# Tokens in two layouts: first blocks scaled by rows in place of transposed, another order of down products, keys in another bank

## The chip, the cores and the metric

The kernel runs on one core of one Trainium2 chip. The metric is the device time of one execution in microseconds (us). Three runs of the kernel before gave 3192.99, 3193.81 and 3198.65 us; their median, 3193.81 us, is the time before.

## The reference

Eight sequences of 512 tokens with 512 features pass through a macaron block: a gated feed-forward part, attention, and the same feed-forward part again, all in float32, with a layernorm ahead of each.

```python
def _layernorm(x, axis=-1, eps=1e-05):
    m = jnp.mean(x, axis=axis, keepdims=True)
    v = jnp.var(x, axis=axis, keepdims=True)
    return (x - m) / jnp.sqrt(v + eps)
...
    h = jax.nn.silu(jnp.einsum('bsh,hi->bsi', x, w_gate)) * jnp.einsum('bsh,hi->bsi', x, w_up)
    h_sparse = _sparsify_2to4(h)
    return jnp.einsum('bsi,ih->bsh', h_sparse, w_down)
...
    x = x + 0.5 * _L0_ffn_ref(_layernorm(x, axis=-1), L0_ffn_w_gate, L0_ffn_w_up, L0_ffn_w_down)
    x = x + _L0_attn_ref(_layernorm(x, axis=-1), L0_attn_W_q, L0_attn_W_k, L0_attn_W_v, L0_attn_W_o)
    x = x + 0.5 * _L0_ffn_ref(_layernorm(x, axis=-1), L0_ffn_w_gate, L0_ffn_w_up, L0_ffn_w_down)
```

The feed-forward part has 2048 hidden features; of each four neighbours the two of largest magnitude are kept. Attention has 16 query heads and 4 key/value heads of 32 features, with rotary positions.

## The kernel before

**Blocks and chunks.** There are 16 feed-forward blocks: for each sequence b a first one (before attention, `i = 0`) and a second one (`i = 1`). `blocks` (L95) gives their order. Places 0 to 3, 5, 8, 9 and 11 are first blocks, whose input is the kernel's own input x. Between the groups of matmuls of a block, "sides" are interleaved: the attention of an earlier sequence and the layernorm of the next block.

A block works through four chunks of 512 hidden features. Per chunk, gate and up are made in two stretches (`woven`, L633) of seven products each instead of eight, in the manner of Strassen and Winograd: the tokens' half blocks `b11`, `b21`, `b22` and four differences of them (`ts`, made by `sums`, L331) are multiplied by quarters of the weights and by sums of quarters. The results are put together in the tiles `row` and `corner`. VectorE then prunes (`keep_two_of_four`, L407; its last step is L454), one half of the tokens after the other. When the second half is done, GpSimd makes three sums `e` and one in place in h (L460 to L463).

Two chunks at a time go through the down projection, again as seven products (`products`, L544, in the order of `PRODUCTS`, L488). Each line of that table names the side taken from h (two digits: token half, feature half) or from e (0, 1, 2), the weights, the accumulating bank (x, v or z), and the quarter of the output that the bank is added to afterwards. A bank goes on accumulating over several products, so a product waits until the add (`add`, L581, operation on L583) that read the bank before it is done. The seven products of a pair of chunks are `owed`, and are worked off at the end of the chunk after it (L777), of the last pair in the first chunk of the next block. `load_x` brings the residual into the only buffer of its pool at the end of a block's first chunk (L778). Three weight tiles are in flight; each product issues the load of the third one after it.

**Layernorm.** `layernorm_t` (L280) is a generator with one step a `yield`. For a first block (tag "xf") it loads four tiles of 128 tokens, takes the moments on VectorE (L297), makes scale and bias in a chain of 12 small operations on GpSimd twice (`scales`, L300), normalises on ScalarE (`normalise`, L314), transposes with 16 TensorE operations in four groups (`turn`, L318; the transposes are on L264), copies the groups from PSUM on ScalarE (L328) and makes the four differences on VectorE (`sums`, on L167). The result `xT` holds features on the partitions and tokens along the row. Only the first block of all has another path (`xb` given).

**What sets the order.** The order of instructions is written out by the program itself under a manual schedule. It keeps a plan of the time at which each engine would be free (`at`), and lets operations of VectorE join a queue: `soon` (urgent), `later` (put off) and the steps of the pruning. `fill` (L388) issues what fits before the planned time of TensorE. A side's next step is taken when its due place has come (`place`, `pace`, L1147 to L1176) and when its condition, the time it yielded, has passed in the plan. `WIDTH`, 42, is the length of a block in those units; a layernorm has 13 steps from 15 to 2 units ahead of its block. Engines execute their queues in order. All transfers are issued by SyncE (SP), also in order; 16 quarters of gate/up weights (`load_quarters`) are in flight.

**PSUM.** Three banks (`Bank`, L227) are shared by all short-lived results: gate/up and down products, transposes (`tr`), key projection (`proj`, L906), values (`vps`, L916) and the softmax denominators. One more bank (`acc_slots`) holds the attention's weighted sums (`ops`, L1071), four a sequence, and another four hold the scores.

Of the kernel before, what the change touches and what calls it, by code (L numbers as in the profile page):

```python
# [18 lines left out]
P = 128  # L19
# [7 lines left out]
def macaron_block(  # L27
    ctx: ExitStack,
    tc: tile.TileContext,
    x: bass.AP,  # L30
    w_gu: bass.AP,
    w_down: bass.AP,
    w_q: bass.AP,
# [74 lines left out]
    def load_quarters(*used):  # L108
# [3 lines left out]
        while coming and len(quarters) < QUARTERS:  # L112
# [4 lines left out]
            elif block != blocks[0]:  # L117
                nc.sync.dma_start(out=w, in_=gu_sums[i][:, q - S1])

    xs = {(0, 0): load_x(0, 0)}  # L120
    load_quarters()
    ident = const.tile([P, P], FP, name="ident")
# [56 lines left out]
    def waits(end):  # L179

        takes("pe", 0.0, end + TOLD)
# [95 lines left out]

    in_xT = []

    def layernorm_t(got, tag, src=None, xb=None):  # L280

# [49 lines left out]
        def sums():  # L331

            xT = got["xT"]
            (b11, b12), (b21, b22) = ([xT[:, 2 * i : 2 * i + 2, j * HALF : (j + 1) * HALF] for j in range(2)] for i in range(2))
            if tag == "xf":
                got["sums"] = ts = tp.tile([P, 4, 2, HALF], FP, tag="ts", name="ts")
            else:
                got["sums"] = ts = p_slots.tile([P, 4, 2, HALF], FP, "ts")
            got["made"] = [
                (later if tag == "xf" else soon)(  # L340
                    0.62, partial(nc.vector.tensor_tensor, ts[:, i], a, b, ALU.subtract), at["act"]
                )
                for i, a, b in ((0, b12, b11), (1, b22, ts[:, 0]), (2, b22, b12), (3, b21, ts[:, 1]))
            ]

        if xb is None:
            there = at["pe"] + 10.0
            yield lambda: there
            found = [soon(0.9, partial(moments, t)) for t in (0, 1)]
            yield now  # L350
            found += [soon(0.9, partial(moments, t)) for t in (2, 3)]
            yield partial(when, found[:2])
            ensure(found[:2])
            scales((0, 1))
            yield partial(when, found)
            ensure(found)
            scales((2, 3))
            yield by_scalar
            for t in range(NT):
                normalise(t)  # L360
                end = at["act"]
                yield by_scalar if t < NT - 1 else (
                    lambda: max(end, by_scalar()) if tag == "xa" or len(in_xT) < 2 else None
                )
            for t in range(NT):
                turn(t)
                yield by_scalar if t < NT - 1 else now
            sums()
        else:

            function(AF.Sqrt)
            for t in range(NT + 1):
                if t < NT:
                    moments(t)
                    va = rs[:, 0, t : t + 1]
                    nc.vector.tensor_scalar(va, mv[:, t, 1:2], EPS, None, ALU.add)
                    nc.scalar.activation(va, va, AF.Sqrt)
                if t:
                    i = t - 1
                    nc.vector.reciprocal(rs[:, 1, i : i + 1], rs[:, 0, i : i + 1])  # L380
                    nc.vector.tensor_scalar(
                        xn[i], xb[:, i, :], mv[:, i, 0:1], rs[:, 1, i : i + 1], ALU.subtract, ALU.mult
                    )
                    turn(i)
            function(AF.Silu)
            sums()
# [88 lines left out]
    def begin(steps):  # L475
# [58 lines left out]
    def ffn(b, final, last):  # L534
# [5 lines left out]
        def store(xb, ts):  # L540
            for t in ts:
                nc.sync.dma_start(out=done[t * P : (t + 1) * P, :], in_=xb[:, t, :])

        def products(hs, g):  # L544
# [8 lines left out]
            def product(i):  # L553
# [37 lines left out]
                written[b, final] = taken[name]  # L591

            for _ in range(3):
                load()
# [38 lines left out]
        def woven(h, i, r, last_one):  # L633
# [95 lines left out]
        for c in range(NCH):  # L729
# [19 lines left out]
            if last and c == NCH - 1:  # L749

                for half in range(2):
                    for r in range(4):
                        yield from hidden(h, 2 * c + r // 2, r, slice(half * HALF, (half + 1) * HALF))
                        if half == 1 and r >= 2:
                            yield from some(2)
                    begin(keep_two_of_four(h, [], e, range(half, half + 1)))
            else:
                for pair in range(2):
# [6 lines left out]
                        groups = woven(h, i, 2 * pair, last_one)  # L765
                    for k, g in enumerate(groups):
                        yield g
                        if k == 2 and opens and i + 1 < 2 * NCH:
                            combine_gu(i + 1)
                    if opens:  # L770
# [64 lines left out]
        return w  # L835

    def attention(b):
        ensure(written[b, 0])
        wkv = wap.tile([P, ND, 2 * KV], FP, tag="wa", name="wkv")
        coming_qo = deque([("q", q) for q in SEVEN_Q] + [("o", q) for q in SEVEN_O])  # L840
        weights = deque()
# [61 lines left out]
                yield partial(when, taken[order[i + 1]] if i < 6 else [])  # L903


        ps = Bank([P, S], "proj")  # L906
        for k in range(ND):
            nc.tensor.matmul(
                out=ps.tile, lhsT=wkv[:, k, :KV], rhs=xT[:, k, :], start=(k == 0), stop=(k == ND - 1)
            )  # L910
        multiplied(3.43)
        fill()
        read, of_k = rotated(kT, ps.tile, cs[:, 0, :], cs[:, 1, :], 1.0)
        ps.free(read)
        yield now
        vps = Bank([P, NT, KV], "vps")  # L916
        for t in range(NT):
# [229 lines left out]
    def place(b, i):  # L1147
        return WIDTH * blocks.index((b, i))
# [116 lines left out]
```

## Time and profile before

| what | value |
|---|---|
| median of three runs | 3193.81 us |
| the profiled execution, its own time | 3194.41 us |
| its span | 3192.6 us |
| granted TensorE clock (mean) | 0.999 |
| TensorE busy, weight loads busy | 3152.0 us, 2391.1 us |
| VectorE, ScalarE, GpSimd busy | 2256.3, 1176.2, 525.6 us |
| DMA: data moved, mean rate | 475.30 MB, 149 GB/s |
| token transposes (L264, float32) | 384 |

The profile describes one execution. Busy time is the time in which an engine had at least one instruction in flight. A matmul's records overlap, so the time that one occupies TensorE is the distance from its start to the start of the next. In a list of waits the columns are: who waited, for whom, the sum, the number of waits and the longest one, in us. In a timeline they are: start, length, engine, line, operation, what it writes and reads, the number of instructions merged, and in brackets the idle time before it with what ended it.

### The profile page before, as it was taken

What the parts mean: (1) busy time and instruction counts of PE and PEld (TensorE: products, weight loads), DVE (VectorE), ACT (ScalarE), POOL (GpSimd) and SP (SyncE); (2) the same over time, 40 slices, a digit from 0 to 9 for tenths busy, and PEclk for the clock granted to TensorE, in tenths of its full rate; (3) what the DMA queues carried; (4) which work ended last, traced back from release to release, by engine and by line L of the source; (5) the groups of instructions that cost most, each with busy time, mean ns of one, the idle gap of its engine ahead of it and who ended that gap; (6) DMA issues with size and microseconds to landing.
All of it is one profiled execution on the core that took longest, in us unless ns stands there. A gap on an engine that the chain in (4) does not pass through costs nothing.

```text
span 3192.6 us, 43897 instructions
## 1 busy us (share of the span) xinstructions
PE 3152.0 (99%) x16264; PEld 2391.1 (75%) x16264; DVE 2256.3 (71%) x4458; ACT 1176.2 (37%) x1663; POOL 525.6 (16%) x822
## 2 busy tenths in 40 slices
PE   8999999999999999999999999999999999999999
PEld 6888667866787668766786678766876678667886
DVE  7767777588658776777658865877577766877554
ACT  2222443235422463244423542255324432454220
POOL 2322011211021102201121112111120112111110
PEclk9999999999999999999999999999999999999999
DMA  7773344534444436334453345443633445334541
GB/s 238 241 262 117 115 152 143 173 123 123 159 156 146 134 107 219 114 116 153 142 175 122 118 161 158 146 135 110 219 114 113 159 139 171 122 123 159 162 165 53
DMA packets 270069, 475.30 MB, mean 149 GB/s; under 512 B 26656, under 2 KB 82464, under 8 KB 269344
## 3 DMA queue, kind: packets, MB, share of 16 engines
q1 hardware_dynamic: 269856, 472.49, 46.4%
q8 instruction: 130, 2.13, 0.3%
q14 instruction: 83, 0.68, 0.1%
HBM read 432.54 MB, written 39.85 MB: 148 GB/s over the span
## 4 chain that ended last, share of the span: by engine, by line
PE 92%; DVE 4%; DMA 2%; POOL 1%; ACT 1%; issue 0%; SPq 0%; DVEq 0%; POOLq 0%; ACTq 0%
PE x L644 25%; PE v L644 13%; PE x L569 13%; PE v L569 7%; PE z L644 6%; PE seven L889 6%; PE st L1002 4%; PE sc L969 4%; PE ops L1018 4%; PE z L569 3%; PE tr L264 1%; PE gu L619 1%; PE vps L919 1%; PE den L1034 1%; PE st L1007 1%; PE y L602 1%
## 5 line engine op out<-in xcount | busy, mean ns | idle before, releaser
L644 PE MATMUL x<-ts,w 128*128 128x256 f32 x3000 | 717.1, 382 | 1.4 <-DVE corner L658 1.3
L644 PEld LDWEIGHTS x<-ts,w 128*128 128x128 f32 x3000 | 560.4, 190 | 130.5 <-issue 41.7
L460 POOL TENSOR_TENSOR e<-h 128x512 f32<-128x512 f32 x62 | 80.3, 1295 | 2154.4 <-DVE h L454 1982.8
L167 DVE TENSOR_REDUCE nm<-sc 128x1 f32<-128x512 f32 x512 | 321.6, 683 | 72.4 <-PE sc L969 70.8
L569 PE MATMUL x<-wd,h 128*128 128x256 f32 x1488 | 340.1, 382 | 0.8 <-DVE x L583 0.8
L569 PEld LDWEIGHTS x<-wd,h 128*128 128x128 f32 x1488 | 279.4, 190 | 61.6 <-issue 14.2
L167 DVE TENSOR_TENSOR total<-total,p 128x512 f32<-128x512 f32 x384 | 271.6, 743 | 73.0 <-ACT p L1010 73.0
L1010 ACT ACTIVATE p<-st 128x2048 f32<-128x2048 f32 x96 | 179.8, 1872 | 330.4 <-PE st L1007 289.5
L244 ACT COPY row<-x 128x512 f32<-128x512 f32 x203 | 118.8, 585 | 405.0 <-PE x L644 404.6
L256 ACT ACT_TABLE_LOAD x195 | 250.2, 1283 | 4.2 <-PEq L1254 0.7
L569 PE MATMUL v<-wd,e 128*128 128x256 f32 x992 | 230.3, 384 | 14.8 <-POOL e L460 11.5
L644 PE MATMUL v<-xT,w 128*128 128x256 f32 x1000 | 239.5, 382 | 2.9 <-ACT corner L244 1.5
L644 PE MATMUL x<-xT,w 128*128 128x256 f32 x1000 | 239.5, 382 | 1.8 <-ACT xT L328 1.8
L644 PE MATMUL z<-xT,w 128*128 128x256 f32 x1000 | 238.6, 381 | 0.0
L644 PE MATMUL v<-ts,w 128*128 128x256 f32 x1000 | 238.2, 381 | 0.0
L693 ACT ACTIVATE h<-x 128x256 f32<-128x256 f32 x125 | 47.6, 381 | 498.9 <-PE x L644 467.9
L569 PEld LDWEIGHTS v<-wd,e 128*128 128x128 f32 x992 | 187.2, 191 | 57.5 <-POOL e L460 14.7
L644 PEld LDWEIGHTS v<-xT,w 128*128 128x128 f32 x1000 | 186.7, 190 | 49.4 <-ACT row L244 8.0
L644 PEld LDWEIGHTS x<-xT,w 128*128 128x128 f32 x1000 | 186.2, 190 | 46.9 <-issue 20.6
L644 PEld LDWEIGHTS z<-xT,w 128*128 128x128 f32 x1000 | 187.1, 190 | 39.0 <-issue 15.0
L644 PEld LDWEIGHTS v<-ts,w 128*128 128x128 f32 x1000 | 187.6, 190 | 38.0 <-issue 8.9
L415 ACT ACTIVATE a<-h 128x1024 f32<-128x1024 f32 x128 | 134.9, 1054 | 159.5 <-DVE m L434 89.9
(129 smaller groups left out, 4564.6 us busy)
## 6 DMA issues: line engine op xcount, KB each, us to landing
w<-gu SPq DMA_DIRECT2D x472, 256.0 KB, 3.5
w<-in_w_gu SPq DMA_DIRECT2D x394, 256.0 KB, 3.4
wd<-wd SPq DMA_DIRECT2D x124, 512.0 KB, 5.4
wd<-in_w_down SPq DMA_DIRECT2D x186, 256.0 KB, 3.7
x<-x SPq DMA_DIRECT2D x64, 256.0 KB, 2.7
xn<-x SPq DMA_DIRECT2D x64, 256.0 KB, 4.5
x<-in_x SPq DMA_DIRECT2D x32, 256.0 KB, 3.6
gu<-w SPq DMA_DIRECT2D x32, 256.0 KB, 2.8
```

The lines of the kernel that those rows point to most:

```text
L167: self.does()
L244: nc.scalar.copy(dst, src)
L256: nc.scalar.activation(dummy[:, 1:2], dummy[:, 0:1], f)
L415: nc.scalar.activation(a, h[:, :, half * HALF : (half + 1) * HALF], AF.Abs)
L460: nc.gpsimd.tensor_tensor(sums[:, 0], h21, h22, ALU.add)
L569: nc.tensor.matmul(out=y.tile[:, t, :], lhsT=part[:, t * P : (t + 1) * P], rhs=operands[i][:, n, :], start=(first and t == 0 and n == 0), ...
L644: nc.tensor.matmul(out=bank.tile[:, m, :], lhsT=lhs[:, m, k, :], rhs=rhs[:, k, :], start=(first and m == 0 and k == 0), stop=(k == 1), ski ...
L889: nc.tensor.matmul(out=sc[:, bank, m, :], lhsT=lhs(w, i, m, k), rhs=rhs(w, i, k), start=(i in (0, 1, 5) and m == 0 and k == 0), stop=(k == 1),
L969: nc.tensor.matmul(out=sc[:, kv, :], lhsT=qT[rows, c, t * P : (t + 1) * P], rhs=kT[rows, :], start=True, stop=True)
L1002: nc.tensor.matmul(out=st[:, kv, :], lhsT=kT[rows, t * P : (t + 1) * P], rhs=qT[rows, c, :], start=True, stop=False)
L1010: nc.scalar.activation(p, st, AF.Exp)
L1018: nc.tensor.matmul(out=ops[rows, :], lhsT=v[:, t, rows], rhs=p[:, kv, :], start=(t == 0), stop=(t == NT - 1))
```

## The change

1. The host gives the input a second time, transposed (`x_t`: features on partitions, tokens along the row). The layernorm of the seven first blocks behind the very first one loads its token tiles for the moments as before, but no longer normalises and transposes them. It stores scale and bias per token in DRAM (`scales_of`, single elements of 4 bytes), loads `xT` from `x_t`, loads the 512 scales and the 512 biases back as rows copied to all 128 partitions, and lets VectorE multiply and add in place, eight operations of 128x512. These layernorms run four units earlier (`AHEAD`).
2. In `PRODUCTS` the product "12" x "21" moves from the sixth place to the second. The stores of a finished output half follow the fifth and the seventh product.
3. Six of the seven owed products are worked off at the end of a chunk; the seventh comes after the first gate/up product of the next stretch. The residual is loaded a chunk later.
4. The key projection goes to the accumulation bank in place of one of the three shared banks.

```diff
+    scales_of = {b: dram.tile([2, S], FP, name=f"scales_{b}") for b in range(B)}
...
+        def given_transposed():
+
+
+            yield lambda: at["pe"] if len(in_xT) < 2 else None
+            for i in range(2):
+                nc.sync.dma_start(out=scales_of[b][i].rearrange("(t p) -> p t", p=P), in_=rs[:, 1 + 2 * i, :])
+            in_xT.append(got)
+            got["xT"] = xT = xtp.tile([P, ND, S], FP, tag="xT", name="xT")
+            for c in range(ND):
+                nc.sync.dma_start(out=xT[:, c, :], in_=x_t[b][:, c, :])
+            there = at["pe"] + 5.0
+            yield lambda: there
+            rows = [xnp.tile([P, S], FP, tag=tag, name="rows") for _ in range(2)]
+            for i in range(2):
+                nc.sync.dma_start(out=rows[i], in_=scales_of[b][i].partition_broadcast(P))
+            there = at["pe"] + 5.0
+            yield lambda: there
+            got["normed"] = []
+            for c in range(ND):
+                got["normed"] += [
+                    later(0.62, partial(nc.vector.tensor_tensor, xT[:, c, :], xT[:, c, :], rows[i], op))
+                    for i, op in enumerate((ALU.mult, ALU.add))
+                ]
+                yield partial(when, got["normed"][-2:])
+            sums()
+            yield partial(when, got["made"])
+            yield now
...
             scales((2, 3))
+            if b is not None:
+                yield from given_transposed()
+                return
             yield by_scalar
...
         ("11", "11", "x", (0, 0)),
+        ("12", "21", "z", (0, 0)),
         (0, "12-11", "v", (1, 1)),
...
         ("21", "22-12", "x", (1, 1)),
-        ("12", "21", "z", (0, 0)),
         ("22", "21-T2", "x", (1, 0)),
...
-                    if g == NCH // 2 - 1 and i in (5, 6):
-                        store(xb, (0, 1) if i == 5 else (2, 3))
+                    if g == NCH // 2 - 1 and i in (4, 6):
+                        store(xb, (0, 1) if i == 4 else (2, 3))
...
+            waits(ensure(normed[b, final].pop("normed", ())))
             x = Bank([P, 2, HALF], "x")
...
                     for k, g in enumerate(groups):
                         yield g
+                        if k == 0 and len(owed) == 1:
+
+                            yield from some(1, False)
...
-                        yield from some(7, False)
-            if c == 0 and (b, final) not in xs:
+                        yield from some(6, False)
+            if c == 1 and (b, final) not in xs:
...
-        ps = Bank([P, S], "proj")
+        ps = acc_slots.tile([P, S], FP, "proj")
+        waits(acc_slots.ready)
...
-        ps.free(read)
+        acc_slots.used(read[0])
...
+    AHEAD = 4
...
-        stage = partial(layernorm_t, normed[b, i], "xf", tokens[b][2 * i])
-        sides.append((place(b, i) - 15, place(b, i) - 2, NORM, stage, ("attention", b) if i else None, None))
+        stage = partial(layernorm_t, normed[b, i], "xf", tokens[b][2 * i], b=None if i else b)
+        ahead = 0 if i else AHEAD
+        sides.append((place(b, i) - 15 - ahead, place(b, i) - 2 - ahead, NORM, stage, ("attention", b) if i else None, None))
...
+        "x_t": x.reshape(B, S, D // P, P).transpose(0, 3, 2, 1),
```

More of the change, by code (lines that the diff above doesn't have):

```diff
@@ L30, in macaron_block @@
     x: bass.AP,
+    x_t: bass.AP,
     w_gu: bass.AP,
@@ L278, in macaron_block, with layernorm_t @@
     in_xT = []
-    def layernorm_t(got, tag, src=None, xb=None):
+    def layernorm_t(got, tag, src=None, xb=None, b=None):
         if tag == "xf":
@@ L340, in sums @@
                 (later if tag == "xf" else soon)(
-                    0.62, partial(nc.vector.tensor_tensor, ts[:, i], a, b, ALU.subtract), at["act"]
+                    0.62, partial(nc.vector.tensor_tensor, ts[:, i], a, a2, ALU.subtract), at["act"]
                 )
-                for i, a, b in ((0, b12, b11), (1, b22, ts[:, 0]), (2, b22, b12), (3, b21, ts[:, 1]))
+                for i, a, a2 in ((0, b12, b11), (1, b22, ts[:, 0]), (2, b22, b12), (3, b21, ts[:, 1]))
             ]
+        def given_transposed():
[23 more added lines that the diff above has]
+            yield now
         if xb is None:
@@ L590, in product @@
                     y.free(taken[name])
-                written[b, final] = taken[name]
+                if i == len(PRODUCTS) - 1:
+                    written[b, final] = taken[name]
             for _ in range(3):
@@ L753, in ffn @@
                         yield from hidden(h, 2 * c + r // 2, r, slice(half * HALF, (half + 1) * HALF))
+                        if half == r == 0:
+                            yield from some(1, False)
                         if half == 1 and r >= 2:
@@ L767, in ffn @@
                         yield g
+                        if k == 0 and len(owed) == 1:
+                            yield from some(1, False)
                         if k == 2 and opens and i + 1 < 2 * NCH:
@@ L775, in ffn @@
                         begin(keep_two_of_four(h, list(last_one), e))
-                        yield from some(7, False)
-            if c == 0 and (b, final) not in xs:
+                        yield from some(6, False)
+            if c == 1 and (b, final) not in xs:
+                assert not owed
                 for entries in written.values():
@@ L837, in attention @@
     def attention(b):
-        ensure(written[b, 0])
+        ensure(written.pop((b, 0)))
         wkv = wap.tile([P, ND, 2 * KV], FP, tag="wa", name="wkv")
@@ L903, in seven @@
                 yield partial(when, taken[order[i + 1]] if i < 6 else [])
-        ps = Bank([P, S], "proj")
+        ps = acc_slots.tile([P, S], FP, "proj")
+        waits(acc_slots.ready)
         for k in range(ND):
             nc.tensor.matmul(
-                out=ps.tile, lhsT=wkv[:, k, :KV], rhs=xT[:, k, :], start=(k == 0), stop=(k == ND - 1)
+                out=ps, lhsT=wkv[:, k, :KV], rhs=xT[:, k, :], start=(k == 0), stop=(k == ND - 1)
             )
@@ L912, in attention @@
         fill()
-        read, of_k = rotated(kT, ps.tile, cs[:, 0, :], cs[:, 1, :], 1.0)
-        ps.free(read)
+        read, of_k = rotated(kT, ps, cs[:, 0, :], cs[:, 1, :], 1.0)
+        acc_slots.used(read[0])
         yield now
```

## The prediction

> **What bounds the kernel now.** I read the page's busy times and its chain first. They say whether a change must take work from TensorE or may only shift it.
>
> ```profile
> span 3192.6 us, 43897 instructions
> ...
> PE 3152.0 (99%) x16264; PEld 2391.1 (75%) x16264; DVE 2256.3 (71%) x4458; ACT 1176.2 (37%) x1663; POOL 525.6 (16%) x822
> ...
> PE 92%; DVE 4%; DMA 2%; POOL 1%; ACT 1%; issue 0%; SPq 0%; DVEq 0%; POOLq 0%; ACTq 0%
> ```
>
> TensorE is busy 99% of the span and is 92% of the chain, at a granted clock of 0.999. A microsecond of matmul time removed is a microsecond of span, unless a new wait takes its place. VectorE (71%) and ScalarE (37%) lie beside it. Second, the waits of TensorE, longest sums first:
>
> ```profile
> PE v L569 <- POOL e L460: 11.5, 8, 2.0
> PE tr L264 <- DVE xn L381: 7.6, 3, 6.5
> PE v L569 <- DMA wd<-in_w_down: 3.2, 1, 3.2
> PE st L1002 <- DVE nm L167: 3.1, 4, 1.8
> PE vps L919 <- DVE kT L167: 2.4, 3, 0.8
> PE x L644 <- ACT xT L328: 1.8, 2, 0.9
> ```
>
> All listed waits add up to 36 us. The largest is the second down product, which needs e, GpSimd's sum, made by L460. The 7.6 us are the program's start, which the change leaves alone. Third, the timeline shows the price of what is removed, and then one of the eight waits for e:
>
> ```profile
> 132.10 0.60 PE L264 MATMUL tr<-ident,xn 128*128 128x128 f32 x4
> 132.54 1.89 PE L644 MATMUL z<-xT,w 128*128 128x256 f32 x8
> 134.27 0.60 PE L264 MATMUL tr<-ident,xn 128*128 128x128 f32 x4
> 134.70 1.89 PE L644 MATMUL x<-ts,w 128*128 128x256 f32 x8
> ```
>
> Matmuls are pipelined, so I go by start to start, not by the 0.60 shown: four transposes hold TensorE for 0.44 us (132.10 to 132.54) and 0.43 us (134.27 to 134.70). A gate/up product takes 1.73 us in the same way (132.54 to 134.27), a down product 3.45 us (its 16 records start at 901.16, the next at 904.62).
>
> ```profile
> 365.00 1.03 PE L569 MATMUL v<-wd,e 128*128 128x256 f32 x4
> 365.09 1.43 DVE L454 SCALAR_TENSOR_TENSOR h<-m,h 128x256 f32<-128x256 bf16 x4
> 366.66 1.26 POOL L460 TENSOR_TENSOR e<-h 128x512 f32<-128x512 f32 x1 [67.90 <-DVE h L454]
> 367.98 2.86 PE L569 MATMUL v<-wd,e 128*128 128x256 f32 x12 [1.96 <-POOL e L460]
> ```
>
> TensorE has done the four records that read the older chunk and waits for the newer chunk's first sum: VectorE ended its pruning (L454) at 366.5, GpSimd took 1.26 us.
>
> **The change, part by part.**
>
> *Transposes.* The built program's order holds 272 token transposes for 384: 7 blocks x 16 are gone, 28 groups of four. 28 x 0.4375 us (mean of the four groups between 131 and 142 us) = **-12.2 us**, all on TensorE. Nothing covers them today, so nothing is kept back. On ScalarE 28 normalisations (L315, 807 ns) and 28 copies (L328, about 586 ns) go, 39 us off the path. At 927 us TensorE waits 0.9 us for such a copy in a window where a first block's transposes stand: **-0.9** (bounds -0.9 and 0). The other 0.9 stands among transposes that stay.
>
> *Order of down products.* ("12","21") moves from sixth to second, so e is needed one product later, 3.45 us. The longest of the eight waits is 2.0 us, so all are covered: **-11.5 us**. "12" reads h12, which neither GpSimd's sums nor the second half of the pruning touches, so it waits for nothing new. Bounds: -11.5, and 0 if pruning itself falls back by as much. Raw and summed weights are loaded in another order. The 3.2 us wait at 107.9 us is a weight load issued at 101.3, behind four sum stores, four xn loads and four gate/up loads. The xn loads now go out four groups earlier (AHEAD), which takes 1.9 us of issue from ahead of it, but the 1.5 us that TensorE lost to e just before is no longer there to help it. I take **-1.5** (bounds -3.2 and 0).
>
> *The last product.* It now stands behind the next stretch's first gate/up product. The product before it uses the same bank x, so its add (L583, 0.69 us) must end within 1.73 us, where z's 3.45 us stood between. I listed the 31 groups' "21" product beside its add in the timeline: in 24 the add ends 0.73 us after the modelled end of the matmuls, in 29 within 1.4, and two come at 1.55 and 2.79. The next start is 1.5 us after that end, so two waits, 0.05 and 1.25 us: **+1.3** (bounds 0 and +8; the third product's adds, the worst placed but the first, would cost 7.7 by the same sum).
>
> *Keys in the accumulation bank.* vps waits for the rotation's reader of the projection's bank three times: **-2.4** (bounds -2.4 and 0). The new bank's last reader is the previous attention's division, 69 us or more before it by the timeline, so no wait takes its place. If that cover went, it would be one VectorE operation, 0.7 us an attention.
>
> *Scaling by rows.* Each of 7 stages adds to VectorE eight multiplications or additions (128x512 f32, both inputs in SBUF). Nearest row: ts<-xT, L167, 681/686/1750 ns least, median, most. The most comes beside GpSimd:
>
> ```profile
> 241.98 1.59 POOL L461 TENSOR_TENSOR e<-e,h 128x512 f32<-128x512 f32 x1
> 242.37 1.75 DVE L167 TENSOR_TENSOR ts<-xT 128x512 f32<-128x512 f32 x1
> 243.65 1.59 POOL L462 TENSOR_TENSOR e<-h,e 128x512 f32<-128x512 f32 x1
> 244.04 1.75 DVE L167 TENSOR_TENSOR ts<-xT,ts 128x512 f32<-128x512 f32 x1
> ```
>
> 56 x 0.69 = 39 us if none collides, 56 x 1.75 = 98 us if all do: 5.5 to 14 us a stage. In the seven windows where these stages run, VectorE is busy 319.9 of 429 us and GpSimd 130.4, so there is some 16 us of room a window, and about three in ten operations meet GpSimd.
>
> This is the rule of the Trainium skill that speaks against the change: "SBUF — State Buffer", section "Who interferes with whom", says that a VectorE instruction with two SBUF inputs contends with a GpSimd instruction that reads SBUF, and whichever starts first holds the port for its whole length. The 1.75 us above agree. By the rule at its worst the stage takes 14 us and nearly fills the window's room; by the median row it takes 5.5.
>
> What decides the cost is not the sum but whether VectorE, which runs in order, stops at the first multiplication for its rows. Before it stand the second GpSimd chain (12 operations, 487.32 to 492.16, some 5 us), the store of the scales, xT's four loads and the two row loads, with at least 5 us of TensorE time planned from store to row load and again from row load to use. Stores of 256 KB land in 2.0 to 2.8 us, xn loads in 2.7/4.5/10.5 (least, median, most). So 5 us cover the median of each hop, and not the slow ones. Bounds a stage: 0, as for the moments (idle before L297: 0.0 with a 10 us lead; a gain is not in it, since ScalarE, the engine relieved, ends only the waits counted above); 4.7 us of stopped VectorE, with GpSimd 6 us late (one chain of e in front), a landing of 2.8 (3.8 over the 5 us) and a row load of 5.9, the slowest median (0.9 over). TensorE outlasts some 1.5 us of such a stop, the slack of a 1.73 us product, so it would lose 3.2, or 22 us over seven. I take 0.5 a stage, **+3.5**, nearer nothing, because xT and rows come when the group's last weight load is already out.
>
> The Trainium skill, "DMA: Bandwidth & Descriptors", section "Rules for kernel authors", adds that a transfer whose last dimension is strided becomes one descriptor an element; the scales' store is one, 512 elements of 4 bytes. No run here prices it yet.
>
> *SP.* 56 more transfers. xn loads take 0.38 us of issue each, so eight are some 3 us a stage. All scale stores stand behind the last weight load of the group's seven products (read in the order of the built program), and gate/up quarters are 16 ahead, 16 x 1.73 = 28 us. So a stop there is hidden: **0**; without that cover, 3 us plus the wait for GpSimd, up to 9 us a stage.
>
> **Sum.** Against the profiled execution's own 3194.4 us (span 3192.6 and 1.8 around it): -12.2 -0.9 -11.5 -1.5 -2.4 +1.3 +3.5 = -23.7, so 3170.7. The median of the runs is 3193.8, 0.6 lower, which I leave out.
>
> **The rivals.**
> 1. *All of the gain, no new wait:* 3194.4 -12.2 -0.9 -11.5 -3.2 -2.4 = 3164.2. For: VectorE has room. Against: the 1.73 us window and the 5 us leads.
> 2. *The wait for e stays:* the added work pushes pruning back and GpSimd's sum is as late as now. 3170.7 + 11.5 = 3182.2. For: in the line above L454 is the releaser, so VectorE is the late one. Against: every wait is under 3.45 us.
> 3. *Rows are late, in part:* 22 us instead of 3.5, 3189.2, no change that could be told. For: xn loads of up to 10.5 us. Against: the medians.
> 4. *Rows are late, and it is slower.* Place: VectorE's queue at the first multiplication, everything behind it (adds, pruning, maxima) stopped for d us in each of seven stages. Price 7 x (d - 1.5) against a gain of 27.2 (the sum without the 3.5): it equals the gain at d = 5.4 and is slower by 0.2% from d = 6.3. At d = 8: 3167.2 + 45.5 = 3212.7. For: two hops through DRAM, the first of single elements. Against: the same round trip by 256 KB tiles takes 7.3 us by the medians (2.8 and 4.5), and 10 are planned.
> 5. *That it doesn't do what it says* is excluded for the transposes by the count; for the waits it is rival 2.
>
> **How the numbers follow.** What a measurement here can tell from no change is about 0.2%, 6.4 us, so the borders are 3187.4 and 3200.2. Forecast (3166 to 3178) 0.58; rival 1 0.13; rival 2 0.13; rival 3 0.08; rival 4 0.08. Faster: 0.58 + 0.13 + 0.13 = 0.84; same 0.08; slower 0.08. The range goes from just under rival 1, with both xT waits gone, 3163, to 3186, beyond rival 2 and short of rival 3.
>
> **What would show it.** Right: 272 transposes, PE busy about 12 us less; no row "v <- POOL e" among TensorE's waits, none "vps <- kT"; L583's add before the last product a wait of 1 to 2 us in all; VectorE idle before xT<-xT,rows near nothing. Wrong: tens of us of idle VectorE released by the rows' DMA (rivals 3 and 4), TensorE waiting for e or for h in the new second product (rival 2), or quarters (w) that TensorE waits for, which I cost at nothing.

## The result and the profile after

| | before | after |
|---|---|---|
| median of 21 runs each | 3196.58 us (3192.99 to 3199.1) | 3200.26 us (3197.32 to 3207.62) |
| the profiled execution, its span | 3194.41, 3192.6 us | 3199.26, 3197.5 us |
| granted TensorE clock (mean) | 0.999 | 0.995 |

The changed kernel takes 1.0013 times as long, 95% interval 1.0007 to 1.0019: slower by 0.13%, within the 0.2% that the prediction counts as no change. The forecast of 3170.7 us, with its range of 3163 to 3186, was wrong. The page of the kernel after, with the lines that answer to those shown before:

```profile
span 3197.5 us, 43783 instructions
...
PE 3147.0 (98%) x16152; PEld 2387.0 (75%) x16152; DVE 2289.0 (72%) x4509; ACT 1137.1 (36%) x1600; POOL 527.2 (16%) x822
...
PE 90%; DVE 4%; DMA 4%; POOL 1%; issue 1%; SPq 0%; ACT 0%; DVEq 0%; ACTq 0%; POOLq 0%
```

The work did go: 112 TensorE instructions fewer, 16264 - 16152, which are the transposes. But TensorE is busy only 5.0 us less, where 12.2 us of transposes (the prediction's price for them) were taken out, and the DMA share of the chain has gone from 2% to 4%. TensorE's waits say where the first of it went (columns: who waited, for whom, sum, number, longest, in us):

```profile
PE x L680 <- DVE corner L694: 9.3, 4, 5.5
...
PE sc L1013 <- DVE nm L170: 6.1, 1, 6.1
PE st L1046 <- DVE nm L170: 4.8, 4, 1.8
PE v L604 <- POOL e L496: 4.4, 2, 2.4
PE v L604 <- POOL e L495: 3.0, 1, 3.0
PE z L680 <- DVE x L618: 2.2, 1, 2.2
```

Lines have moved: L604 is the old L569 (down products), L680 the old L644 (gate/up), L618 the old L583 (the add), L694 the old L658, L495 and L496 the old L460 and L461. The row for kT is gone, as forecast. Three long waits for VectorE are new, and by this list e, which was to be covered, still holds TensorE for 4.4 + 3.0 = 7.4 us. What VectorE itself waited for is told by the view of the tile `rows`, the scales and biases loaded back as rows:

```profile
L170 DVE TENSOR_TENSOR xT<-xT,rows x56: 681/689/1746, 127.6 to 2188.2; 128x512 f32<-128x512 f32 x56
...
its engine sat idle before it (us, times) until:
  DMA rows<-scales: 30.0, 6
...
DMA to landing us min/median/max: 4.3/6.7/7.7
```

VectorE stood still for 30.0 us at six of the 56 operations, the first multiplication of six stages (a stage is the layernorm of one first block): 8.7 us at 127.6, 8.0 at 303.5, 1.6 at 518.0, 7.5 at 930.7, 2.3 at 1555.6 and 1.9 at 2174.0. The operations themselves are cheap (median 689 ns); they started late. The view of DMA issues (how many, KB each, median us from issue to landing) names the hop that is slow:

```profile
xn<-in_x SPq DMA_DIRECT2D x28, 256.0 KB, 5.3
xT<-in_x_t SPq DMA_DIRECT2D x28, 256.0 KB, 12.4
...
rows<-scales SPq DMA_DIRECT2D x14, 256.0 KB, 6.7
...
scales<-rs SPq DMA_DIRECT2D x14, 2.0 KB, 10.9
```

The smallest transfer of the kernel, 2 KB in 512 elements of 4 bytes, lands in 10.9 us, longer than any 256 KB load but one, and that one, xT, is issued directly behind it. Against 5 us planned for this hop and 5 us for the next stand 10.9 and 6.7. The timeline of one stage shows how it reaches TensorE (start, length, engine, line, operation, number merged, and in brackets the idle time before it and its releaser):

```profile
286.59 0.94 SPq L355 DMA_DIRECT2D scales<-rs  x2
...
287.62 1.89 SPq L359 DMA_DIRECT2D xT<-in_x_t  x4
...
296.75 1.11 SPq L364 DMA_DIRECT2D rows<-scales  x2
...
303.47 1.42 DVE L170 TENSOR_TENSOR xT<-xT,rows 128x512 f32<-128x512 f32 x2 [7.96 <-DMA rows<-scales]
304.81 2.48 DVE L170 TENSOR_REDUCE nm<-sc 128x1 f32<-128x512 f32 x4
...
307.34 2.09 PE L1013 MATMUL sc<-kT,qT 32*128 32x512 f32 x8 [6.11 <-DVE nm L170]
```

The store goes out at 286.59, the row load 10.2 us later, as soon as the store has landed, and the rows land after another 6.7 us. VectorE's queue had reached the multiplication at 295.5 and stood for 7.96 us. Behind it stood the maxima of the attention's scores (nm), which TensorE needed before it could overwrite their bank: 6.11 us. In the same way the rows cost TensorE 2.23 us at 131.9 (an add), 5.47 us at 140.1 and 3.32 us at 937.8 (corners): 17.1 us in four waits. The 5.47 us hold more than the stop: beside GpSimd's sums e, four of the stage's operations took 6.45 us (131.76 to 138.21), where four at the median take 2.8. In experiment 4 below the same four took 6.10 us, VectorE had not been stopped before them, and TensorE did not wait.

The last part was on no list of the prediction: the granted clock. The view of windows (window, its length, then busy time and number for PE, PEld, DVE, ACT, POOL, then the clock, DMA share and GB/s) for every stretch after the first 20 us in which it was below full:

```profile
102.30:105.70 3.40, 2.79 (x7) 2.25 (x8) 3.40 (x3) 0.00 (x0) 3.24 (x3) 0.51 1.04 395
133.10:143.30 10.20, 4.73 (x12) 3.29 (x11) 8.65 (x10) 0.00 (x0) 4.49 (x3) 0.50 0.57 193
303.80:310.50 6.70, 3.16 (x11) 1.48 (x12) 5.65 (x10) 0.00 (x0) 0.00 (x0) 0.50 0.00 2
488.10:491.40 3.30, 3.30 (x9) 2.55 (x9) 3.19 (x5) 0.00 (x0) 1.66 (x2) 0.50 0.19 58
938.70:942.00 3.30, 3.30 (x12) 2.66 (x11) 2.05 (x5) 1.06 (x3) 0.00 (x0) 0.50 0.02 5
1525.80:1529.00 3.20, 3.20 (x9) 2.57 (x8) 3.20 (x5) 0.00 (x0) 0.93 (x1) 0.50 0.05 18
```

Every one of the six begins during a TensorE wait of 2 us or more, or within 1.3 us of its end. In 20.48 us of TensorE's busy time the clock was half, so half of it, 10.2 us, was lost; the kernel before had one such window, at 108.1 us, worth 1.7 us. These 8.5 us more cover the 7.2 us by which TensorE's busy time fell less than 12.2.

The account, my sum from both traces: transposes -12.2; TensorE's gaps over 0.15 us, without the program's first wait, +10.0 (30.1 us before, 40.1 after); half clock +8.5. That is +6.3, where the spans differ by +4.9; 1.4 us of it stays unexplained.

### The profile page after: what moved, and what is told of

It is laid out like the page before. It is cut to its first block, busy times and chain, and to the rows that moved or that the text cites. A ratio compares the mean times of both kernels' runs of the same rounds, so it can differ in the third digit from the quotient of the medians.

```text
span 3197.5 us, 43783 instructions
## 1 busy us (share of the span) xinstructions
PE 3147.0 (98%) x16152; PEld 2387.0 (75%) x16152; DVE 2289.0 (72%) x4509; ACT 1137.1 (36%) x1600; POOL 527.2 (16%) x822
## 4 chain that ended last, share of the span: by engine, by line
PE 90%; DVE 4%; DMA 4%; POOL 1%; issue 1%; SPq 0%; ACT 0%; DVEq 0%; ACTq 0%; POOLq 0%
PE x L680 26%; PE v L680 13%; PE x L604 11%; PE z L680 6%; PE v L604 6%; PE seven L932 6%; PE sc L1013 4%; PE st L1046 4%; PE ops L1062 4%; PE z L604 3%; DMA scales<-rs 2%; PE gu L655 1%; PE tr L267 1%; DMA rows<-scales 1%; PE vps L963 1%; PE den L1078 1%
## 5 line engine op out<-in xcount | busy, mean ns | idle before, releaser
L680 PE MATMUL x<-ts,w 128*128 128x256 f32 x3000 | 719.0, 383 | 9.4 <-DVE corner L694 9.3
L680 PEld LDWEIGHTS x<-ts,w 128*128 128x128 f32 x3000 | 563.6, 191 | 133.3 <-issue 38.3
L495 POOL TENSOR_TENSOR e<-h 128x512 f32<-128x512 f32 x62 | 81.2, 1309 | 1926.0 <-DVE h L489 1743.1
L604 PE MATMUL x<-wd,h 128*128 128x256 f32 x1488 | 338.8, 381 | 1.8 <-DVE st L301 1.2
L604 PEld LDWEIGHTS x<-wd,h 128*128 128x128 f32 x1488 | 280.4, 190 | 55.2 <-issue 11.4
L680 PE MATMUL v<-ts,w 128*128 128x256 f32 x1000 | 241.0, 384 | 1.9 <-ACT xT L332 1.3
L680 PE MATMUL v<-xT,w 128*128 128x256 f32 x1000 | 239.6, 382 | 3.3 <-DVE corner L249 1.8
L680 PE MATMUL z<-xT,w 128*128 128x256 f32 x1000 | 239.8, 383 | 2.2 <-DVE x L618 2.2
L680 PE MATMUL x<-xT,w 128*128 128x256 f32 x1000 | 239.8, 383 | 0.9 <-ACT xT L332 0.9
L604 PE MATMUL v<-wd,e 128*128 128x256 f32 x992 | 231.6, 387 | 7.5 <-POOL e L496 4.4
L604 PEld LDWEIGHTS v<-wd,e 128*128 128x128 f32 x992 | 189.7, 193 | 49.3 <-issue 9.1
L680 PEld LDWEIGHTS v<-ts,w 128*128 128x128 f32 x1000 | 186.6, 190 | 53.3 <-issue 23.6
L680 PEld LDWEIGHTS v<-xT,w 128*128 128x128 f32 x1000 | 187.0, 190 | 51.3 <-issue 9.6
L680 PEld LDWEIGHTS x<-xT,w 128*128 128x128 f32 x1000 | 186.9, 190 | 47.1 <-issue 20.8
L680 PEld LDWEIGHTS z<-xT,w 128*128 128x128 f32 x1000 | 187.4, 190 | 44.2 <-issue 16.8
L489 DVE SCALAR_TENSOR_TENSOR h<-m,h 128x256 f32<-128x256 bf16 x512 | 190.7, 421 | 0.0
```

Of the source, the lines that this page charges most:

```text
L489: nc.vector.scalar_tensor_tensor(hh[:, r, :], s, n, hh[:, r, :], op, ALU.mult)
L495: nc.gpsimd.tensor_tensor(sums[:, 0], h21, h22, ALU.add)
L604: nc.tensor.matmul(out=y.tile[:, t, :], lhsT=part[:, t * P : (t + 1) * P], rhs=operands[i][:, n, :], start=(first and t == 0 and n == 0), ...
L680: nc.tensor.matmul(out=bank.tile[:, m, :], lhsT=lhs[:, m, k, :], rhs=rhs[:, k, :], start=(first and m == 0 and k == 0), stop=(k == 1), ski ...
```

## Experiments

Each ratio is against the kernel before, run on the same chip in the same session.

**1. The orders alone.** All layernorms by transposes again; order and split of the down products and the keys' bank as after.

```diff
-    AHEAD = 4
+    AHEAD = 0
...
-        stage = partial(layernorm_t, normed[b, i], "xf", tokens[b][2 * i], b=None if i else b)
+        stage = partial(layernorm_t, normed[b, i], "xf", tokens[b][2 * i], b=None)
```

> The order of down products, the split seventh product and the keys' bank alone; tokens of first blocks are transposed as before (384 transposes). Theory (the loss of the whole change comes from the scaling by rows: VectorE stopped 30.0 us at the rows, GpSimd's scale chains run ahead of e, and the clock halves after waits of 2 us and more): no wait for e, none for kT, no half-clock window beyond the one near 108 us, and 10 to 14 us less than before. Rival (the new order itself loses what it gains, by the 1.73 us window before the last product): within 3 us of before, with 8 us or more of waits of down products for L618's adds.

Measured: 3185.24 us against 3195.46, ratio 0.9969 (0.9957 to 0.9981). TensorE's waits:

```profile
PE x L604 <- DMA wd<-wd: 5.1, 1, 5.1
...
PE x L604 <- DVE x L618: 1.8, 1, 1.8
```

No row for e and none for kT is left, and the moved last product waits once, 1.8 us. The new order does what it was forecast to do; the weights' wait grew from 3.2 to 5.1 us. So three of the four parts are a gain of some 10 us, and the loss comes with the rows.

**2. The rows alone.** Scaling by rows and AHEAD kept; order of products, six of seven owed, load of the residual and keys' bank as before.

```diff
-        ("12", "21", "z", (0, 0)),
         (0, "12-11", "v", (1, 1)),
...
+        ("12", "21", "z", (0, 0)),
         ("22", "21-T2", "x", (1, 0)),
...
-                        yield from some(6, False)
+                        yield from some(7, False)
...
-        ps = acc_slots.tile([P, S], FP, "proj")
+        ps = Bank([P, S], "proj")
```

> The scaling by rows alone, with its four units' earlier start; products, owed products, residual load and keys' bank as before. Theory: VectorE stops some 25 to 35 us at the rows, e is waited for more than before (over 11.5 us, since the scale chains come ahead of e on GpSimd and the second product needs e), five or more half-clock windows; 5 to 20 us slower than before in spite of 112 transposes fewer. Rival (the interplay of the parts loses, not the rows): faster than before by 8 to 12 us.

Measured: 3224.17 us against 3195.46, ratio 1.0092 (1.0077 to 1.0107): 28.7 us slower, where 5 to 20 were expected. The tile `rows` had 29.2 us of stopped VectorE in six places, as after; the rest is in TensorE's waits:

```profile
PE v L604 <- POOL e L495: 20.3, 10, 6.5
PE x L679 <- DVE corner L693: 9.4, 2, 8.1
```

The waits for e have grown (before: 11.5 us in 8, longest 2.0). The timeline at 97 us shows why for the longest:

```profile
97.18 0.28 POOL L308 TENSOR_SCALAR rs<-mv 128x2 f32<-128x2 f32 x1
...
101.79 0.67 POOL L316 TENSOR_SCALAR rs<-rs 128x2 f32<-128x2 f32 x1
102.42 1.26 POOL L495 TENSOR_TENSOR e<-h 128x512 f32<-128x512 f32 x1
...
103.73 0.80 PE L604 MATMUL v<-wd,e 128*128 128x256 f32 x1 [6.46 <-POOL e L495]
```

GpSimd, in order, works through the chain of 12 small operations (97.2 to 102.5) and only then makes e. AHEAD moved the whole layernorm earlier, its GpSimd chain too, and that chain now stands ahead of e. In the kernel after the same happens at 96.2 us, and TensorE waits 3.01 us, until 102.91: the new order of products gives 3.45 us of cover, which the chain eats up.

The other two waits for e of the kernel after, 2.39 us at 487.8 and 2.06 us at 1524.8, have another cause. The first of them:

```profile
482.93 1.42 DVE L489 SCALAR_TENSOR_TENSOR h<-m,h 128x256 f32<-128x256 bf16 x4
483.16 0.27 POOL L316 TENSOR_SCALAR rs<-rs 128x2 f32<-128x2 f32 x1
...
484.51 1.31 POOL L495 TENSOR_TENSOR e<-h 128x512 f32<-128x512 f32 x1 [1.07 <-DVE z L1026]
484.72 1.16 DVE L1029 CAST z<-nm 128x16 bf16<-128x16 f32 x1
...
485.90 1.26 POOL L496 TENSOR_TENSOR e<-e,h 128x512 f32<-128x512 f32 x1
485.92 1.28 DVE L1028 TENSOR_TENSOR nm<-nm,z 128x16 f32<-128x16 f32 x1
...
487.32 0.41 DVE L170 TENSOR_TENSOR h<-h,x 128x256 f32<-128x256 f32 x1
...
487.83 4.51 PE L604 MATMUL v<-wd,e 128*128 128x256 f32 x12 [2.39 <-POOL e L496]
```

GpSimd's chain (its last operation is L316) is over at 483.43, and GpSimd stands idle until VectorE's pruning (L489) ends at 484.35. So here e is late because pruning is, the prediction's rival 2, but by little: its first sum (L495) ends 0.4 us after the product before. Nor does the sum that the list names end the wait: L496 ends 0.67 us before TensorE goes on, while every wait for e in the kernel before ended within 0.06 us of its sum. What ends 0.10 us before is `h<-h,x`, the operation that by the program frees a gate/up product's bank. It stood behind small operations of VectorE, two of which took 1.16 and 1.28 us beside GpSimd's e in place of some 0.2. At 1524.8 it is the same, with `h<-h,x` ending 0.10 us before.

The parts are not additive: -10.2 and +28.7 make +18.5, and together they measured +3.7. The waits for e explain little of that: 11.5 us before, none in 1 and 20.3 in 2 would add up to 8.8, and 7.4 were listed. Of the 14 us between sum and whole in the profiles, 6.4 are in TensorE's gaps over 0.15 us, nearly all of it a wait for weights that each part has alone (5.1 us in 1, 4.9 in 2) and both together do not (0.6; before, 3.2). Most of the rest, 7.2 us, is in its busy time; what that comes from stays open.

**3. Rows later, a first attempt.** The stage earlier still, and 15 us of planned time from store to row load.

```diff
-            there = at["pe"] + 5.0
+            there = at["pe"] + 15.0
...
-    AHEAD = 4
+    AHEAD = 13
```

> The whole change, but the layernorms start 13 units early in place of 4 and 15 us in place of 5 are planned between the store of the scales and the load of the rows; the work is the same. Theory: VectorE does not stop at the rows (under 2 us in all), GpSimd's chains are done before e, at most one half-clock window; 3163 to 3175 us. Rival (VectorE's 56 operations more, or their collisions with GpSimd, are the loss): the same 42 us of VectorE work are still there, so the time stays at 3195 or more.

Measured: 3203.72 us against 3195.46, ratio 1.0029 (1.0019 to 1.0039), and VectorE stood 38.2 us at the rows instead of less: a miss of the design. A side that is three units past its due place takes its next step whatever its condition says, so the 15 us made the stage overdue, and the multiplication was issued straight behind the row load: in the longest of the stops VectorE stood from 240.6 to 254.6, and SyncE issued the row load only at 247.1. It doesn't speak for or against the theory, only against a lead that the due places don't leave room for.

**4. Pieces of 16 bytes.** The changed kernel with four neighbouring tokens on a partition, so that a partition's four scales lie side by side in DRAM: the same 2 KB in 128 pieces of 16 bytes. The token tiles are loaded in that order; the moments don't mind.

```diff
-                nc.sync.dma_start(out=xn[t], in_=src[t * P : (t + 1) * P, :])
+                nc.sync.dma_start(out=xn[t], in_=src[t * P : (t + 1) * P, :] if b is None else src.rearrange("(p t) d -> p t d", t=NT)[:, t, :])
...
-                nc.sync.dma_start(out=scales_of[b][i].rearrange("(t p) -> p t", p=P), in_=rs[:, 1 + 2 * i, :])
+                nc.sync.dma_start(out=scales_of[b][i].rearrange("(p t) -> p t", t=NT), in_=rs[:, 1 + 2 * i, :])
```

> The whole change, but a partition takes the moments of four neighbouring tokens, so that its four scales are 16 neighbouring bytes in DRAM: 128 pieces a store in place of 512 of 4 bytes. Theory (the store's 10.9 us come from the number of pieces): the store lands in 3 to 5 us, xT behind it in 5 to 7 in place of 12.4, VectorE stops under 8 us at the rows, and the time falls by 10 to 20 us against the whole change. Rival (the store waits behind earlier transfers or for DRAM, whatever its pieces): it still takes 9 us or more and the time stays.

Measured: 3178.38 us against 3195.46, ratio 0.995 (0.9935 to 0.9964), a little more than the 10 to 20 us expected. The DMA issues:

```profile
xT<-in_x_t SPq DMA_DIRECT2D x28, 256.0 KB, 6.8
...
rows<-scales SPq DMA_DIRECT2D x14, 256.0 KB, 5.4
...
scales<-rs SPq DMA_DIRECT2D x14, 2.0 KB, 4.5
```

The store lands in 4.5 us instead of 10.9, xT behind it in 6.8 instead of 12.4, the token tiles as before (5.2 us), and VectorE stands 4.9 us in three places instead of 30.0. The stage shown above, in this kernel:

```profile
280.30 0.86 SPq L355 DMA_DIRECT2D scales<-rs  x2
281.25 3.18 SPq L359 DMA_DIRECT2D xT<-in_x_t  x4
...
285.51 1.18 SPq L364 DMA_DIRECT2D rows<-scales  x2
...
292.44 2.21 DVE L170 TENSOR_TENSOR xT<-xT,rows 128x512 f32<-128x512 f32 x2 [3.21 <-DMA rows<-scales]
```

From store to row load it takes 5.2 us where it took 10.2. One layout of two transfers is worth 21.9 us (3200.26 to 3178.38, two sessions whose kernels before differ by 1.1 us). The e waits are as they were (3.0 and 4.4 us), so they don't come from the late rows.

**5. Single elements, with time.** The 4-byte store kept; 15 us from store to row load, and due places that leave room for it (steps from 31 to 4 units ahead).

```diff
-            there = at["pe"] + 5.0
+            there = at["pe"] + 15.0
...
-        ahead = 0 if i else AHEAD
+        ahead, sooner = (0, 0) if i else (2, 16)
...
-        sides.append((place(b, i) - 15 - ahead, place(b, i) - 2 - ahead, NORM, stage, ("attention", b) if i else None, None))
+        sides.append((place(b, i) - 15 - sooner, place(b, i) - 2 - ahead, NORM, stage, ("attention", b) if i else None, None))
```

> The whole change with its stores of single elements, 15 us planned from store to row load, and the layernorm's 13 steps spread over 27 units from 31 to 4 ahead of the block, so that no step is overdue (a side's step is taken without regard to its condition when it is 3 units past its due place; in e3 the load of the rows was so late that the first multiplication followed it at once). Theory: the stores still take some 11 us, but nothing waits for them: VectorE stops under 3 us in all, the chains of GpSimd are done before e, at most one half-clock window, 3165 to 3177 us. Rival (the work added to VectorE is the loss): 3195 or more.

Measured: 3196.14 us against 3195.8, ratio 1.0001 (0.9991 to 1.0011), outside what was expected. VectorE stood only 8.7 us at the rows, but TensorE waited 2.76, 4.52, 10.69 and 3.43 us at 65, 77, 107 and 138 us, all within the program's first two blocks. The longest of them comes from the first stage's store, by way of SyncE's queue and not of the rows:

```profile
89.33 10.14 SPq L117 DMA_DIRECT2D w<-in_w_gu  x4
...
105.45 0.69 DVE L750 TENSOR_TENSOR w<-w 128x512 f32<-128x512 f32 x1 [12.00 <-DMA w<-in_w_gu]
...
106.80 1.65 PE L680 MATMUL x<-ts,w 128*128 128x256 f32 x3 [10.69 <-DVE corner L694]
```

Between the first and the second of the four weight loads SyncE stands 6.5 us, until the store has landed; VectorE, whose sums of weights need the last of them, stands 12.0 us. Experiment 8 takes this one stage out.

**6. Pieces of 16 bytes, nine units ahead.** Experiment 4 with `AHEAD = 9` for 4, so that GpSimd's chain, and the moments on VectorE, no longer come just before e.

> e4 (runs of 16 bytes) with the layernorms 9 units early in place of 4, so that GpSimd's two scale chains run before e and not between the pruning and e. Theory: the three waits for e left in e4 (3.0, 2.4 and 2.1 us) go, with the half-clock windows behind two of them: 7 to 11 us less than e4, 3167 to 3172. Rival (e was late because pruning was late): the waits for e stay, and the time stays within 3 us of e4's 3178.4.

Measured: 3174.11 us against 3195.8, ratio 0.9932 (0.9917 to 0.9948), 3170.6 to 3178.07 in its four runs: the lowest median of the study, faster than both kernels. VectorE never stood at the rows, and no e wait is left. But it is 4.3 us less than experiment 4, not the 7 to 11 expected, and the intervals overlap, so the time doesn't show the step from 4 to 9 to be a gain. The profiles, of 6 in its slowest run and of 4 in its fastest, say where the gain went: TensorE's gaps are 3.0 us shorter, but 13.7 us passed at half clock where it was 6.8, behind waits of 2.39, 1.80 and 2.27 us that are not for e.

**7. xT's load at the start of the stage.** Experiment 6, with the four loads of xT ahead of the moments, not behind the store.

```diff
+        if b is not None:
+            assert len(in_xT) < 2
+            in_xT.append(got)
+            got["xT"] = xtp.tile([P, ND, S], FP, tag="xT", name="xT")
+            for c in range(ND):
+                nc.sync.dma_start(out=got["xT"][:, c, :], in_=x_t[b][:, c, :])
...
-            yield lambda: at["pe"] if len(in_xT) < 2 else None
+            yield now
```

> e6 with the loads of xT issued together with the token tiles at the layernorm's start, so that the rows do not come behind xT's 1 MB. Theory: rows land in 3 to 4 us in place of 5.4 and VectorE stops under 1 us at the rows; 0 to 4 us less than e6. Rival: the load at the start collides with others and nothing is gained.

Measured: 3184.6 us against 3195.8, ratio 0.9966 (0.9953 to 0.9979): a miss. Store and rows did land sooner (3.0 and 4.3 us, for 3.9 and 6.4 in experiment 6), but in the first of the stages the store now met GpSimd's scales unfinished, SP waited 7.9 us for them, and the rows came late:

```profile
98.33 0.69 DVE L170 TENSOR_TENSOR xT<-xT,rows 128x512 f32<-128x512 f32 x1 [11.01 <-DMA rows<-scales]
...
100.01 3.78 PE L683 MATMUL x<-ts,w 128*128 128x256 f32 x8 [10.04 <-DVE corner L697]
```

**8, 9, 10. The first stage by transposes.** Experiments 5, 6 and 7 once more, with the layernorm of sequence 1, the first stage, normalised and transposed as before (shown for 9):

```diff
-        stage = partial(layernorm_t, normed[b, i], "xf", tokens[b][2 * i], b=None if i else b)
-        ahead = 0 if i else AHEAD
+        stage = partial(layernorm_t, normed[b, i], "xf", tokens[b][2 * i], b=None if i or b == 1 else b)
+        ahead = 0 if i or b == 1 else AHEAD
```

> e5 with the layernorm of the second block of all (b = 1) by transposes as before, since e5's long stops (10.7, 4.5, 3.4, 2.8 us) all lie before 140 us; the other six keep their stores of single elements, planned 15 us ahead. Theory (the stores harm only where something waits for them): no more than 12 us of waits before 140 us, one half-clock window, 3176 to 3184 us. Rival (single elements or VectorE's added work cost time anywhere): 3190 or more.

> e6 with the layernorm of b = 1 by transposes (16 transposes, 1.75 us, more). Theory: e6's 10 us of waits before 140 us stay about the same (e1 has 10.1 there), so the time is within 4 us of e6's 3174.1. Rival (the scaling in the first block is what remains to be gained): 6 us or more faster than e6.

> e7 with the layernorm of b = 1 by transposes. Theory: e7 lost its time before 140 us alone (VectorE stopped 11.0 us there, behind GpSimd), so without that it is 3171 to 3177, as fast as e9. Rival (early loads of xT cost elsewhere): 3180 or more.

| experiment | before | this | ratio | with the first stage by rows |
|---|---|---|---|---|
| 8 (single elements, time) | 3196.79 | 3177.07 | 0.9945 (0.993 to 0.996) | 3196.14 |
| 9 (16 bytes, nine ahead) | 3196.79 | 3176.96 | 0.9943 (0.9928 to 0.9957) | 3174.11 |
| 10 (16 bytes, xT early) | 3196.79 | 3177.36 | 0.9942 (0.9925 to 0.9959) | 3184.6 |

8 and 9 lie where they were expected, 10 is 0.4 us above. The three can't be told from each other. In 8 the store still lands in 10.1 us, VectorE stands 6.9 us in all, and the kernel is 0.55% faster than before, as fast as 9: what costs is not the slow store but what waits for it. It also clears VectorE's added work, 48 operations of it here, of the loss. For 5 and 7 the whole of what they lost was in the first stage; for 6, whose first stage doesn't wait for its rows, taking it out gains nothing. One loss all three share: near 110 us TensorE waits 5.8 to 6.0 us for weights, with 6.8 us at half clock, where it was 3.2 and 3.4 before.

## Why the prediction was wrong

*The step that failed* is "Scaling by rows", +3.5 us. It measured 17.1 us of waits, plus the half clock behind them: the windows at 133.1, 303.8 and 938.7 us hold 4.73 + 3.16 + 3.30 = 11.2 us of TensorE work, of which half, 5.6 us, was lost. So 22.7 us, by chance just the upper bound of 22 that the step had named, and the step turned out as rival 3 had it. The mechanism, VectorE stopped at the first multiplication, was right, and so was the price of a stop: the formula of rival 4, each stop less 1.5 us, gives 21.0 us for the six stops, where TensorE waited 17.1. The size of the stops was taken at the wrong end, because the store of the scales was priced by the nearest store at hand, 256 KB tiles in 2.0 to 2.8 us, "the same round trip by 256 KB tiles takes 7.3 us". The scales are 512 elements of 4 bytes and took 10.9 us. The likeness that counted here is that of the pieces, not of the bytes: with 128 pieces of 16 bytes, experiment 4, the same 2 KB took 4.5 us. Whether it is the number of pieces or their size, the runs don't tell, since both changed. The page of the Trainium skill that the prediction quoted, "DMA: Bandwidth & Descriptors", section "Rules for kernel authors", says that such a transfer becomes one descriptor an element. The sentence was set down without a price, and nothing was done with it.

*Order of down products*, -11.5 us. The order itself was right: in experiment 1 every e wait is gone. In the kernel after 7.4 us remain, plus half of the 2.79 + 3.30 + 3.20 us in the three windows that they start, 4.6 us, together 12.1 us: all of the gain is given back. What was overlooked is that AHEAD moves all that a stage issues: SP's queue was worked through, and for the scales the chain's 5 us, but not who stands behind the chain on GpSimd. It was e, for 3.0 of the 7.4 us. The other 4.4 come by way of VectorE (experiment 2). With the stage moved earlier still, experiment 6, all three waits are gone.

*The clock* is in no step. Before, one wait of 3.2 us was followed by one window of half clock, and I did not read it. It adds 8.5 us to the kernel after, over a third of the expected gain.

*Right, with their numbers:* the transposes, -12.2 (112 instructions fewer; 6, which has neither late rows nor e waits, is 11.1 us faster than 1, which agrees); the wait for ScalarE's copy of xT, -0.9 (0.9 left of 1.8); the keys' bank, -2.4 (no row left); the last product, +1.3 (1.8 in experiment 1). The weights' wait, -1.5, went further in the kernel after (0.6 us left of 3.2), where an e wait of 3.0 us stands before it and probably gives the load its time, and the other way where no e wait stands there (5.1 in experiment 1, 3.0 in 6, 5.8 to 6.0 in 8 to 10; before, 3.2). SP at 0 holds: SP stood 51.6 us at the row loads, in nine places, and no quarter (w) released TensorE late. In experiment 5, where SyncE stood at the weight loads themselves, it was not free.

*The sum again,* with the terms as measured: -23.7, rows +19.2 more, e and its clock +12.1, weights' wait and its clock window gone -2.8 (3.2 - 0.6 + 1.7 - 1.5), the longer waits of st for nm +1.7 (4.8 for 3.1). That is +6.5, beside a measured +4.9. Without the two causes, in experiment 6, the kernel reaches 3174.1 us against the forecast 3170.7.

*Still open:* which part of the 10.9 us is the store's own and which comes from its place among other transfers. Only the size of the pieces was changed, not the load around them.

## What to carry to other kernels

Price a small transfer by its pieces, and plan its lead by that price: an engine that works in order and meets a DMA that has not landed stops all its later work, the urgent too (VectorE 30.0 us at the rows here, SyncE 6.5 us behind the store in experiment 5). When a stage is moved earlier, list for each engine what now stands behind its instructions; here a 12-operation chain on an engine that is 16% busy cost TensorE 3.0 us at one place, and half clock behind it. And count a TensorE wait of over 2 us at its length plus the clock. Read a releaser against the times beside it: a wait that goes on 0.67 us after the named operation's end was probably ended by something else.

## What the runs showed of the hardware

**Half clock after waits shorter than a window.** In the twelve profiled executions (before, after and the ten experiments) I listed each wait of TensorE over 1 us behind the first 20 us, and whether a stretch at granted clock 0.50 began in it or just behind it. The stretches last 3.4 us or a multiple of it.

| wait | followed by half clock |
|---|---|
| 1.0 to 1.5 us | 0 of 43 |
| 1.5 to 2.0 us | 1 of 34 |
| 2.0 to 2.5 us | 7 of 11 |
| 2.5 to 3.4 us | 6 of 10 |
| over 3.4 us | 17 of 18 |

The one of the last row that no stretch followed lies in a stretch that had already begun.

So a wait of 2 to 3.4 us has an even chance or better to cost 1.7 us more (half of 3.4) than its length. The Trainium skill, "TensorE: Matmul & The Clock Gate", section "HAM oscillation — how this bites in real kernels", gives the rule as no idle gaps over some 3.4 us. Here 13 of 21 waits between 2.0 and 3.4 us already brought the clock down, so by the measurement the line lies near 2 us.

**A scattered store holds up what follows it.** xT's four loads, plain 256 KB transfers on the same queue, landed in 12.4 us behind the 4-byte store and in 6.8 us behind the 16-byte one; the same kernel's token loads took 5.3 and 5.2 us.
